# Expert stages of a four-layer kernel in a written order, two blocks a step, with packed constants

## The chip, the cores and the metric

The kernel runs on one core of one Trainium2 chip. The time is the device time of one execution in microseconds. Engines are named as in the profile: PE multiplies matrices (PEld is its weight load), DVE is the vector engine, ACT the activation engine, POOL the general engine that here mostly issues indirect transfers, SP the engine that issues the other transfers. Three runs of the kernel before took 1355.46, 1358.62 and 1359.36 us; the median is 1358.62 us.

## The reference, cut to what matters

Four layers run over `x` of 4 batches, 512 rows and 128 columns, in float32. Each layer adds an attention to `x` and then a mixture of 8 experts:

```
x = x + L0_xattn(layernorm(x), ctx)        # one similarity map, softmax, 512 -> 128 projection
x = x + L0_ffn(layernorm(x))               # top 2 of 8, silu(x W1 + b1) * (x W0 + b0), then W2
x = x + L1_xattn(ctx, ctx, layernorm(x))   # 16 heads of 8 columns, masked
x = x + L1_ffn(layernorm(x))               # top 1 of 8 with a capacity, gelu, hidden 512
x = x + L2_xattn(layernorm(x), ctx)        # 16 heads of 64 columns, own layernorm and a gate
x = x + L2_ffn(layernorm(x))               # top 2 of 8, gelu, hidden 256, no biases
x = x + L3_xattn(layernorm(x), ctx, ctx)   # 16 heads of 64 columns
x = x + L3_ffn(layernorm(x))               # top 2 of 8, relu, hidden 512
```

The context `ctx` has 154 rows for each batch. A softmax runs over these 154 for each of 16 heads and each row of `x`.

## The kernel before

**Tiles.** The rows are cut into 16 tiles of 128 (4 batches `b`, 4 tiles `i` each). `x` stays on the chip for the whole kernel.

**Attention of layers 1 to 3.** `attend_all` (L1272) runs one period for each tile. A period works on two tiles at once: `new`, whose scores, maxima and exponentials are made, and `old`, the tile before it, whose probabilities are turned (transposed), multiplied by the values, scaled, projected and added to `x`. `narrow_period` (L431) is that of layer 1, `wide_period` (L486) that of layers 2 and 3. The pieces are methods of `Tile` (L267). `score(g)` has PE make scores of six heads (four for the last of the three groups) in a two-bank PSUM tile `sc`. `most(g)` has DVE take the maxima of a group (L292). `exp(g)` has ACT do one exponential with a sum for each head (L304). `turn(n)` is four transposes on PE into a tile `tr`, and `take(n)` the copy out of it (L261 on DVE, L264 on ACT). `by_v` is the product with the values, `inverse` (L326) and `replicate` (L331) make the inverse sums, send them through DRAM and read them back spread over the partitions (`rep`), `scaled` (L411) multiplies by them, `project` (L421) and `residual` end the tile. `parts` are the pieces that prepare the next batch (normalised rows, their transpose, keys, values), `queries` the query projection of the next tile. PSUM has two buffers each of `sc`, `tr` and `av`.

**Routing.** `route` (L647) is a generator. For one half of the rows (two batches, 8 tiles) it normalises, makes the logits, finds the top experts and gives each row a place in a buffer of 128-row blocks sorted by expert; it puts the scatters (one indirect transfer on POOL for each tile and choice, L718) on a list, and then makes the weights and adds the last bias. `row_transfers` issues from that list, two for each `take` or block.

**Experts.** `experts` (L821) is a generator too, over 23 blocks for each half (15 in layer 1). For block `j` it reads the expert's number, loads that expert's first weights with its biases packed behind them (`w`, three buffers, L861), multiplies (`up`, L872), and then finishes the block before it (`down`): activation with bias into `hT` (layer 0: ACT's silu into `eg`, L887, then DVE's product, L888; layer 1 L890; layer 2 L880; layer 3 DVE L894 and ACT L896), second product (L899), copy to `ys` (L907) and store to `ybuf`. Every four blocks the next four blocks of tokens are transposed and copied (`tokens`, L845). After a half's blocks, `gather` (L932) fetches rows back from `ybuf` and `combine` (L950) adds them.

**What sets the order.** Within `with tc.manual_schedule(engines=ordered)`, PE, ACT and DVE keep the order in which the program writes their instructions; SP's and POOL's are placed by a planner. Before, only the attention of layers 1 to 3 stands in that block. The attention of layer 0, the expert stages and the routing in them are placed by the planner on all engines. The main loop (L1313 on) steps the generators by turns: blocks of half 0 beside the routing of half 1, then blocks of half 1 beside the combining of half 0 and the preparation of the next attention.

Of the kernel before, what the change touches and what calls it, by code (L numbers as in the profile page):

```python
# [19 lines left out]
P = 128  # L20
# [6 lines left out]
E = 8  # L27
# [19 lines left out]
def tile_xattn_moe_stack(ctx: ExitStack, tc: tile.TileContext, a: dict, out: bass.AP):  # L47
# [94 lines left out]
    wide_ends = const.tile([P, 4, P], F32, name="wide_ends")  # L142
    nc.gpsimd.memset(wide_ends, 0.0)
# [31 lines left out]
    nth = const.tile([1, BLK[0], E], F32, name="nth")  # L175
# [4 lines left out]
    def row_bc(src, n, name):  # L180

        t = const.tile([P, n], F32, name=name)
        nc.sync.dma_start(t, src.partition_broadcast(P))
        return t


    ctxT = const.tile([P, B, S2], F32, name="ctxT")
    ct4 = const.tile([P, B, 4, ST], F32, name="ct4")
    ct2 = const.tile([P, B, 64], F32, name="ct2")
    nc.gpsimd.memset(ct2, 0.0)  # L190
    tp = ps_tr()
    for b in range(B):
        nc.tensor.transpose(tp[:, b * P : (b + 1) * P], cm[:, b, :], ident)
    nc.vector.tensor_copy(ctxT[:, :, 0:P], tp.rearrange("p (b k) -> p b k", b=B))
    tp = ps_tr()
    for b in range(B):
        nc.tensor.transpose(tp[:, b * ST : (b + 1) * ST], ctail[:, b, :], ident[:ST, :ST])
    tpv = tp[:, 0 : B * ST].rearrange("p (b k) -> p b k", b=B)
    nc.vector.tensor_copy(ctxT[:, :, P:S2], tpv)
# [3 lines left out]

    def columns(src, rows, name):

        t = p2.tile([rows, P], F32, tag="rows", name=f"{name}_r")
        nc.sync.dma_start(t, src)
        q = ps_tr()
        nc.tensor.transpose(q[:, 0:rows], t, ident[:rows, :rows])
        o = const.tile([P, rows], F32, name=name)  # L210
        nc.vector.tensor_copy(o, q[:, 0:rows])
        return o
# [54 lines left out]
    class Tile:  # L267
# [8 lines left out]
        def __init__(self, at, i):  # L276
            self.at, self.i = at, i
            self.per = P // at.dh
            self.nb = H // self.per
            self.pr = p2.tile([P, H, S2], F32, tag="probs", name="probs")  # L280
# [31 lines left out]
        def short(self):  # L312
            if self.nb == 1:
                self.ends = p2.tile([P, 4, T4], F32, tag="short", name="short", bufs=1)
                nc.scalar.copy(self.ends.rearrange("p g (h k) -> p (g h) k", h=4), self.pr[:, :, P:S2])
            else:
                self.ends = wide_ends
# [38 lines left out]
        def take_ends(self, engine):  # L356
            self.tails = p2.tile([self.rows, 4, P], F32, tag="tails", name="tails")
            copy(engine, self.tails.rearrange("p g q -> p (g q)"), self.q["ends"][0 : self.rows, :])
# [1028 lines left out]
```

## Time and profile before

| | |
|---|---|
| median of three runs | 1358.62 us |
| profiled execution | 1354.62 us |
| its span, first to last instruction | 1352.8 us |
| mean granted clock of PE | 0.930 |
| PE / PEld busy | 1113.4 / 908.6 us |
| DVE / ACT / POOL busy | 770.9 / 568.8 / 252.9 us |
| transferred | 126.81 MB, mean 94 GB/s |

Read as stages, the span falls into: attention of layer 0 up to 94 us, a wait for scattered rows up to 117, experts of layer 0 up to 293, attention 1 up to about 511, experts 1 up to 605, attention 2 up to about 846, experts 2 up to 955, attention 3 up to about 1199, experts 3 up to 1325, and the last gather up to 1352.8. Busy times of an engine are of its instructions alone; a matmul record's end is modelled.

### The profile page before, as it was taken

The page shows a single profiled execution, that of the slowest core. Times are in us where ns is not written, and L with a number is a line of the kernel's source. Part 1 is how long each engine was busy: PE and PEld are TensorE (multiplying, and loading weights), DVE is VectorE, ACT ScalarE, POOL GpSimd, SP SyncE. Part 2 cuts the span into 40 slices and gives each one's busy share as a digit, 9 for nine tenths or more (in the row PEclk, how much of TensorE's full clock was granted, in tenths as well). Part 3 has the DMA queues.
Part 4 walks back from the last instruction along what each step waited for, and adds up shares of the span by engine and source line. Part 5 has one row for each costly group of instructions (what it writes and reads, how often), then busy time and mean ns, then how long its engine had stood idle before and what let it go on. Part 6 is the DMA issues. An engine that isn't in the chain of part 4 may idle for free.

```text
span 1352.8 us, 26947 instructions
## 1 busy us (share of the span) xinstructions
PE 1113.4 (82%) x9435; PEld 908.6 (67%) x9435; DVE 770.9 (57%) x2089; ACT 568.8 (42%) x2258; POOL 252.9 (19%) x281
## 2 busy tenths in 40 slices
PE   4885988887777788889999988868899998889891
PEld 3775887764334347777778777756777777679881
DVE  5563645557766764245666776425477576646452
ACT  1112443455454444455555455212555555433230
POOL 2022213104000020312000003045120000402424
PEclk8786998999898988998999999879999999989996
DMA  7013675551101214532112213444421111335762
GB/s 216 0 63 107 184 232 153 167 170 40 21 19 28 63 40 112 147 108 79 33 33 55 57 36 105 114 147 129 126 60 43 33 33 33 86 82 146 203 186 61
DMA packets 136995, 126.81 MB, mean 94 GB/s; under 512 B 13466, under 2 KB 116511, under 8 KB 136479
## 3 DMA queue, kind: packets, MB, share of 16 engines
q1 hardware_dynamic: 129695, 110.39, 29.4%
q0 software_dynamic: 7168, 14.69, 3.6%
q8 instruction: 78, 1.28, 0.4%
q14 instruction: 54, 0.44, 0.1%
HBM read 101.31 MB, written 23.72 MB: 92 GB/s over the span
## 4 chain that ended last, share of the span: by engine, by line
PE 35%; DVE 8%; DMA 6%; ACT 4%; issue 4%; POOL 3%; SPq 0%; POOLq 0%; DVEq 0%; ACTq 0%
PE sc L605 5%; PE tr L421 5%; PE av L404 4%; PE tr L367 4%; PE sc L872 4%; DMA w<-in_up 3%; PE av L899 3%; PE sc L590 3%; ACT probs L304 2%; DVE nm L292 2%; PE av L386 2%; DVE pT L261 2%; POOL yg L932 1%; PE sc L554 1%; POOL buf L718 1%
## 5 line engine op out<-in xcount | busy, mean ns | idle before, releaser
L304 ACT ACTIVATE probs<-sc,nm 128x154 f32<-128x154 f32 x768 | 286.1, 404 | 266.1 <-DVE nm L292 265.8
L872 PE MATMUL sc<-tokT,w 128*128 128x128 f32 x1528 | 213.9, 289 | 29.2 <-DMA w<-in_up 22.8
L872 PEld LDWEIGHTS sc<-tokT,w 128*128 128x128 f32 x1528 | 192.9, 200 | 43.3 <-issue 11.4
L899 PE MATMUL av<-w,hT 128*128 x1160 | 175.0, 284 | 11.4 <-DVE hT L888 8.5
L292 DVE TENSOR_REDUCE nm<-sc 128x6 f32<-128x924 f32 x144 | 142.9, 1009 | 68.1 <-PE sc L605 34.0
L304 ACT ACTIVATION_READ_ACCUMULATOR probs<-sc,nm 128x1 f32 x768 | 170.2, 222 | 0.0
L899 PEld LDWEIGHTS av<-w,hT 128*128 128x128 f32 x1160 | 150.4, 194 | 23.0 <-DVE hT L888 12.7
L932 POOL DMA_INDIRECT yg<-ybuf,su x112 | 107.6, 960 | 277.6 <-DVE pT L261 132.6
L261 DVE COPY pT<-tr 128x512 f32<-128x512 f32 x192 | 128.0, 687 | 52.3 <-PE tr L367 49.3
L233 POOL TENSOR_TENSOR rstd<-ve,nhalf 128x4 f32<-128x4 f32 x32 | 32.9, 1030 | 652.7 <-DVE ve L231 598.6
L718 POOL DMA_INDIRECT buf<-xn,su x112 | 108.1, 965 | 163.5 <-DVE eb L741 42.1
L367 PE MATMUL tr<-ident,probs 128*128 128x128 f32 x768 | 117.2, 287 | 13.3 <-DVE pT L261 13.3
L367 PEld LDWEIGHTS tr<-ident,probs 128*128 128x128 f32 x768 | 84.9, 144 | 40.3 <-DVE pT L261 20.4
L404 PE MATMUL av<-pT,vm 128*64 128x128 f32 (+1 forms) x1536 | 104.8, 286 | 7.1 <-DVE pT L261 7.1
L887 ACT ACTIVATE eg<-sc,w 128x128 f32<-128x128 f32 x184 | 66.2, 367 | 94.5 <-DVE hT L888 72.7
L907 DVE COPY ys<-av 128x128 f32<-128x128 f32 x168 | 48.5, 289 | 82.8 <-PE av L899 75.5
L888 DVE SCALAR_TENSOR_TENSOR hT<-sc,w,eg 128x128 f32<-128x128 f32 x184 | 63.0, 348 | 51.2 <-ACT eg L887 48.6
L404 PEld LDWEIGHTS av<-pT,vm 128*64 128x64 f32 (+1 forms) x1536 | 65.0, 128 | 35.9 <-issue 20.5
L605 PE MATMUL sc<-kT,qT 64*128 64x154 f32 x1024 | 85.1, 304 | 3.5 <-ACT probs L304 3.5
L605 PEld LDWEIGHTS sc<-kT,qT 64*128 64x128 f32 x1024 | 69.8, 186 | 13.3 <-ACT probs L304 7.7
L421 PE MATMUL tr<-wo,aT 128*128 128x128 f32 x512 | 67.1, 284 | 9.3 <-ACT tails L264 6.8
L590 PE MATMUL sc<-xnT,wq 128*128 128x128 f32 x512 | 71.0, 296 | 2.9 <-ACT probs L304 2.9
(251 smaller groups left out, 1460.6 us busy)
## 6 DMA issues: line engine op xcount, KB each, us to landing
w<-in_up SPq DMA_DIRECT2D x46, 516.0 KB
w<-in_up SPq DMA_DIRECT2D x76, 258.0 KB
rep<-rd SPq DMA_DIRECT2D x64, 256.0 KB
ybuf<-ys SPq DMA_DIRECT2D x168, 64.0 KB
tok<-buf SPq DMA_DIRECT2D x36, 256.0 KB
w<-in_down SPq DMA_DIRECT2D x3, 2048.0 KB
w<-in_up SPq DMA_DIRECT2D x46, 128.0 KB
buf<-zero SPq DMA_DIRECT2D x2, 1472.0 KB
```

The costliest lines, as they stand in the source:

```text
L261: return nc.vector.tensor_copy(o, i)
L292: nc.vector.tensor_reduce(self.at.heads(self.nm, g, n), self.sc[g][:, :, 0 : n * S2].rearrange("p j (s k) -> p j s k", s=n), AX.X, ALU.max ...
L304: nc.scalar.activation(self.pr[:, h, :], self.sc[g][:, j, s * S2 : (s + 1) * S2], AF.Exp, bias=self.nm[:, h : h + 1], accum_out=self.rs[:, ...
L367: nc.tensor.transpose(q[:, t * P : (t + 1) * P], self.pr[:, h, 0:P], ident)
L404: nc.tensor.matmul(av[rows, cols], v, self.pT[n][:, t, :], start=False, stop=last)
L421: nc.tensor.matmul(o[:, 0:D], self.aT[:, c, :], self.at.wo[:, c, :], start=(c == 0), stop=(c == self.nb - 1))
L590: nc.tensor.matmul(sc[:, c // 4, c % 4 * P : (c % 4 + 1) * P], wq[:, c * P : (c + 1) * P], at.xnT[:, i * P : (i + 1) * P], start=True, sto ...
L605: nc.tensor.matmul(sc[:, j, s * S2 : (s + 1) * S2], at.qT[i][rows, c, :], at.kT[rows, c, :], start=True, stop=True)
L718: ins = nc.gpsimd.indirect_dma_start(out=buf[half], out_offset=bass.IndirectOffsetOnAxis(ap=su[:, t : t + 1], axis=0), in_=xns[t // NI][:, ...
L872: nc.tensor.matmul(dst, w[:, at : at + P], xT, start=True, stop=True)
L899: nc.tensor.matmul(y[:, 0:D], hT[:, fc, :], w2[:, bass.ds(e, 1), fc, :].rearrange("p o d -> p (o d)"), start=(fc == 0), stop=(fc == nf - 1),)
L932: ins = nc.gpsimd.indirect_dma_start(out=yg[:, t, :], out_offset=None, in_=ybuf[half], in_offset=bass.IndirectOffsetOnAxis(ap=su[:, t : t ...
```

## The change

1. All of the main loop after the attention of layer 0 now stands in the block of the written order: the expert stages, the routing beside them, and the preparation of the next attention.
2. `experts` works on steps of two blocks in layers 1 to 3 (one in layer 0). Weights have four buffers of a step and are loaded three steps ahead. In a step the written order is: load, `up` of this step, `down` of the step before with its copy to `ys` (on ACT in layer 0, on DVE otherwise), activation of this step, and every four blocks the token transposes and their copy. In layer 3 the first block's relu is DVE's and the second block's ACT's.
3. Biases are no longer loaded with the weights. `route` picks each block's biases out of a table on the chip, by a mask and sum over experts on DVE. The weights and the last bias of a half become a second generator, `weigh`; for half 1 of layers 0 to 2 it runs in the next attention.
4. Small constants are packed on the host into a few arrays, the context is also passed transposed, and the transposes that made columns of them on the chip are gone.
5. `narrow_period`: the scores and maxima of group 0 of the next tile are made near the end of the period, after `parts` and before `inverse`; both first exponential groups stand together; `after` ends the period.
6. `wide_period`: the projection comes before the turning of the ends, and turn 0 of the new tile is done at the end of its own period with its copy on ACT.
7. Buffers: `probs`, `rep` and `tails` become single (probs in two halves), `w` has four, `hT` four, `ys` two.

```diff
...
         if new:
-            new.score(0)
             new.score(1)
         if old:
             old.turn_ends()
-        if new:
-            new.most(0)
-        if old:
             old.turn(0)
         if new:
             new.most(1)
             new.exp(0)
+            new.exp(1)
         if old:
             old.take_ends("v")
+            old.take(0, "v")
             old.by_v_ends()
-            old.take(0, "v")
             old.turn(1)
             old.take(1, "v")
+        if new:
+            new.score(2)
+        if old:
             old.turn(2)
             old.by_v(0)
             old.by_v(1)
         if new:
-            new.score(2)
-            new.exp(1)
-        if old:
-            old.take(2, "v")
-        if new:
             new.most(2)
             new.exp(2)
         if old:
+            old.take(2, "v")
             old.turn(3)
+            old.by_v(2)
             old.take(3, "v")
-        middle()
-        if old:
-            old.by_v(2)
             old.by_v(3)
             old.scaled(0)
+        middle()
+        parts()
+        if nxt:
+            nxt.score(0)
+            nxt.most(0)
         if new:
             new.short()
             new.inverse()
         queries()
         if new:
             new.replicate()
-        parts()
-        after()
         if old:
             old.project()
             old.residual()
+        after()
...
-            for n in range(3):
+            for n in (1, 2):
                 old.turn(n)
                 old.take(n, "v")
...
             old.by_v(3)
+            old.scaled(1)
         middle()
-        if old:
-            old.scaled(1)
...
             new.replicate()
-            new.turn_ends()
-            new.take_ends("s")
-        after()
         if old:
             old.project()
             old.residual()
+        if new:
+            new.turn_ends()
+            new.take_ends("s")
+            new.turn(0)
+            new.take(0, "s")
+        after()
...
+        if layer != 2:
...
+            begun = rt.tile([P, BLK[0], E], F32, tag="begun", name="begun", bufs=1)
+            nc.vector.tensor_tensor(begun[:, 0:nj, :], bc(first, 1, nj), nth[:, 0:nj, :], ALU.is_le)
+            nc.vector.tensor_tensor(begun[:, 0:nj, :], begun[:, 0:nj, :], past[:, 0:nj, :], ALU.subtract)
+            yield
...
+            for c in range(nc_):
...
+                nc.vector.tensor_tensor(t8[:, 0:nj, :], begun[:, 0:nj, :], bc(biases[layer][:, c, :], 1, nj), ALU.mult)
+                nc.vector.tensor_reduce(r.biases[:, 0:nj, c], t8[:, 0:nj, :], AX.X, ALU.add)
+                if c % 4 == 3 and c < nc_ - 1:
+                    yield
...
+                    if layer == 0:
+                        g = p2.tile([P, P], F32, tag="eg", name="eg", bufs=4)
+                        nc.scalar.activation(g, sc[:, 1, cols], AF.Silu, bias=bcol[:, j, nf + fc : nf + fc + 1])
+                        nc.vector.scalar_tensor_tensor(hT[:, fc, :], sc[:, 0, cols], b0, g, ALU.add, ALU.mult)
+                    elif layer == 1:
+                        nc.scalar.activation(hT[:, fc, :], sc[:, n, cols], AF.Gelu, bias=b0)
+                    elif n == 0:
+                        nc.vector.tensor_scalar(hT[:, fc, :], sc[:, n, cols], b0, 0.0, ALU.add, ALU.max)
+                    else:
+                        nc.scalar.activation(hT[:, fc, :], sc[:, n, cols], AF.Relu, bias=b0)
...
+            row_transfers(
+                2 * per, copy("s" if layer == 0 else "v", ys[:, 0:m, :].rearrange("p n d -> p (n d)"), y[:, 0 : m * D])
             )
...
+        for n, blocks in enumerate(steps):
+            j = blocks[0]
+            load_up(n + 3)
+            sc = up(blocks, ws.pop(n))
             if last:
                 down(*last)
-            last = this
+            last = blocks, activate(blocks, sc)
             if j % 4 == 2 and j // 4 + 1 in loaded:
                 tokens(j // 4 + 1)
                 load(j // 4 + 2)
             yield
...
+    with tc.manual_schedule(engines=ordered):
+        for layer in range(4):
+            if layer:
+                routed, last, weights = attend_all(layer, prepare, found, at, beside)
+            row_transfers()
+            pace = (1, 3, 2, 2)[layer]
+            first = Steps(experts(layer, 0, routed, weights)).step()
+            if last:
+                (narrow_period if layer == 1 else wide_period)(None, last)
+            if layer < 3:
+                prepare = setups[layer + 1]()
+            second = Steps(routing(layer, 1, layer == 3))
+            while not first.done:
+                first.step()
+                second.step(pace)
+            behind = second.finish()
+            row_transfers()
+            got = gather(0, routed, first.result)
+            second = Steps(experts(layer, 1, behind, weights))
+            while rows_due:
+                second.step()
+            second.step()
+            onto = Steps(onward(layer, 0, routed, got, prepare, found))
+            while not second.done:
+                second.step()
+                onto.step(pace)
+            at = onto.finish()
+            beside = Steps(finishing(behind, gather(1, behind, second.result)))
         row_transfers()
```

## Prediction

> **What bounds the kernel now.** I first read busy time by stage. The columns are the stretch and its length in us, then PE, PEld, DVE, ACT and POOL busy with their instructions, PE's granted clock, the DMA share and GB/s.
>
> ```profile
> 117.00:293.00 176.00, 157.20 (x1228) 145.36 (x1226) 96.39 (x320) 75.89 (x198) 33.03 (x34) 0.97 0.58 175
> 293.00:511.00 218.00, 166.22 (x1318) 84.48 (x1319) 147.30 (x334) 111.35 (x537) 28.25 (x29) 0.91 0.15 43
> 511.00:605.00 94.00, 83.26 (x676) 76.17 (x676) 34.98 (x123) 43.01 (x135) 18.42 (x19) 0.95 0.46 130
> 605.00:846.00 241.00, 215.66 (x2154) 179.86 (x2151) 161.21 (x344) 130.96 (x588) 28.14 (x29) 0.99 0.23 56
> 846.00:955.00 109.00, 83.70 (x570) 73.23 (x569) 41.04 (x147) 26.18 (x61) 33.80 (x35) 0.86 0.45 130
> 955.00:1199.00 244.00, 218.52 (x2159) 181.61 (x2157) 160.48 (x341) 130.75 (x587) 35.88 (x37) 0.98 0.22 58
> 1199.00:1325.00 126.00, 115.46 (x940) 107.17 (x940) 63.73 (x220) 34.60 (x107) 31.80 (x33) 0.99 0.59 160
> ```
>
> Experts 0 to 3 take 176, 94, 109 and 126 us, the attentions between them 218, 241 and 244. PE is busy about nine tenths of each except attention 1 and experts 2, where most room is. Then the waits: who waited, for whom, total us, times, longest.
>
> ```profile
> ACT eg L887 <- DVE hT L888: 72.7, 130, 4.0
> ...
> ACT hT L896 <- DVE hT L894: 54.3, 33, 6.0
> ...
> PE tr L845 <- DMA tok<-buf: 33.3, 7, 15.9
> PE tr L331 <- DVE rinv L326: 32.0, 29, 2.9
> PE sc L872 <- DMA w<-in_up: 22.8, 31, 2.2
> PE av L380 <- DVE tails L261: 18.6, 15, 4.7
> ```
>
> The last four are PE's own and can be won or lost directly; 15.9 us of L845 is the wait for scatters before experts 0. The first two show ACT and DVE taking turns on one `sc` tile. The timeline (start, us, engine) shows it in a block of layer 0:
>
> ```profile
> 143.28 0.37 ACT L887 ACTIVATE eg<-sc,w 128x128 f32<-128x128 f32 x1 [0.43 <-DVE hT L888]
> ...
> 143.68 0.35 DVE L888 SCALAR_TENSOR_TENSOR hT<-sc,w,eg 128x128 f32<-128x128 f32 x1 [0.43 <-ACT eg L887]
> ...
> 144.07 0.37 ACT L887 ACTIVATE eg<-sc,w 128x128 f32<-128x128 f32 x1 [0.42 <-DVE hT L888]
> ...
> 145.63 0.29 DVE L907 COPY ys<-av 128x128 f32<-128x128 f32 x1
> ```
>
> A turn takes 144.07 − 143.28 = 0.79 us. The next silu waits for the product although it needs only another column of `sc`. The copy to `ys` at 145.63 is DVE's, slipped in while ACT has the tile.
>
> [...] granted clocks of 0.86 in experts 2 and 0.91 in attention 1, the stages with most idle PE, against 0.98 and 0.99 in attention 3 and 2, agree.
>
> **The change, part by part**, against the profiled execution's 1354.6 us (span 1352.8), 0.3% under the median of 1358.6.
>
> *Experts 0: +14.* In written order ACT does copy n−1 to `ys` before the silus of block n, and that copy waits for the second product, which waits for the last `hT`. A block's loop is: three turns 3 × 0.79, then silu 0.37, gap 0.03, product 0.35: 3.12. From last `hT` to copy 0.24 (142.45 to 142.69 in the timeline). ACT's copy of 128x128: no such row; 128x208 took 0.38 (L319) and DVE's 0.29, so I take 0.30, bounds 0.26 and 0.39. Sum 3.66; 46 blocks 168.5. Before, steady blocks lasted 3.0 to 3.1 (starts 149.41, 152.49, 155.47), PE's own work: 16 records of L872 in 2.0, 8 of L899 in 1.0, a share of the token transposes. Around the loop: routing and bias pieces on DVE beyond the slack left in a block (statistics 2.7, norm 2.2, bias sums of 0.32 + 0.31 each) about 6.5, two starts of a half 5.4, end 1, preparing attention 1 2, PE's clock at the two starts about 6. Together 190 against 176. The new weight ring and `eg`'s four buffers hold nothing here: loads come three steps ahead, and the 6.8 us that PE waited for `w` in this stage go.
>
> *Attention 1: +11.* PE's transpose of the sums (L331, first instruction of `replicate`) now stands behind `most(0)` of the next tile and `inverse` on DVE. The maximum of six narrow heads takes 1.12, the inverse 0.25, and with 0.18 for the passing of signals the wait is 1.55 a tile; before it was 18.3 in 15 tiles of this stage, 1.2: +5 over 15. `parts` and `middle`, DVE pieces of 0.2 to 1.4 us, now stand ahead of L331 too, where PE has little but the scores of group 0 to do: I take 0.5 a tile, +8 (bounds 0 and 20). The weights of half 1 move in, with 3 us of PE's work and waits. At L380 the product of the ends waits for `tails` behind one maximum fewer on DVE, but PE has one group of scores less to cover it: of 18.6 I take a quarter back, −5 (bounds 0 and 18.6). `exp(0)` and `exp(1)` side by side cost nothing while ACT is busy 111 of 218; without that cover a group of six exponentials, 6 × 0.4, would stand in each tile.
>
> *Experts 1: 0.* 30 blocks at 2.0 of PE are 60; tokens 3.7, their waits 5, the old tile's period 8, routing 3.5, in-order stalls 6 (three pieces a step, so a norm on DVE and its transpose on PE fall in one step), next attention's pieces 7.7: 94, as before.
>
> *Attentions 2 and 3: −4 and −10.* Projection ahead of the turning of the ends removes PE's wait for ACT's copy at L421 (4.1 + 0.7 and 2.7 + 1.4), and turn 0, moved to the end of its own period, takes away part of L367's waits for L261 (7.0 and 6.2; I take 2.5 of the one and, no later piece being in the way in layer 3, 6 of the other; bounds 0 and all). Weights of half 1 bring 3 into attention 2. ACT's added 0.585 a tile lies under its idle time (131 of 241).
>
> *Experts 2: −12.* PE's work is 1.0 a block (four records of L872 and four of L899), 46 in all; tokens 5.7, ten token stalls at 0.9, old tile 9, routing 3.5 + 2.5, next attention's pieces 7.7, border of the halves 10 (16 scatters at 0.965 + 0.30 = 1.27 and the landing, half of it hidden), gathers 3: 97 against 109. PE's 9.7 us for `w` go; the 9.7 for tokens mostly stay.
>
> *Experts 3: +14.* 23 steps at 4.0 are 92; tokens 5.7, old tile 9.5, routing 6.5. Ten token stalls: the copy to `tokT` now stands in its queue behind the copy to `ys` (0.40), four relus on DVE (4 × 0.27 = 1.1) or four on ACT (1.45), and the next `up` waits for it: 1.7 on DVE, 2.8 on ACT, 22 in all; in-order waits at the border 5: 140 against 126.
>
> *No charge:* constants and transposed context (the transposes lie before the first rows are normalised; what else goes lies under 23 us of waiting for scatters with PE busy 2.9); biases of half 0 of layer 0 (5 us of DVE under that wait, DVE busy 5.5 of 23); last gather, 16 × 1.27 on POOL with 8 us around, unchanged; transfers, fewer and of double size, DMA share at most 0.59. The single `rep` and `tails` are read before their next writing in the written order. Scatters and gathers go four a step in layers 1 to 3 against two a block: the same rate on POOL. [...]
>
> Sum in order of time: 14 + 11 + 0 − 4 − 12 − 10 + 14 = +13: 1367.6 beside the profiled execution, 1371.6 beside the median. I take 1371.
>
> **Rivals.**
> A, faster: layer 0's block stays bound by PE at 3.1, because ACT's copy doesn't hold the next silu (PE runs a block ahead, so the wait of the copy ends early). Then 46 × (3.66 − 3.1) = 26 and the 6 of the clock go: about 1340. For it: PE was busy 157 of 176. Against: the copy needs the last product, and the chain of turns alone is 3.12. It decides from a block below 3.38 us, where 46 × 0.28 cancels the 13.
> B, slower still: DVE and ACT pieces meet more waits: copy 0.39 (+4), all token copies on ACT (+6), the clock of 0.91 in experts 0 too (+6), in-order stalls of routing doubled (+8): about 1395.
> C, no change: the token stalls of layer 3 hide under the second block's multiplications, at 2 us a block (14 of the 22 go): 1357.
> That the written order isn't kept is no strong rival: in attention, PE's order in the trace is the written one.
>
> **From the numbers to the chances.** Likeliest 1363 to 1390, 0.48; A 0.24; B 0.20; C 0.08. Faster is A, the same C, slower the rest: 0.24, 0.08, 0.68; three runs spread by 0.3%, which is about what a measurement of this kernel can tell from no change. The range 1332 to 1404 reaches over A and B with the bounds of the copy (46 × 0.13 = 6), of half clocks and stalls, and leaves out what lies past either.
>
> **What would show it.** Right: in experts 0, silus of successive blocks start 3.6 to 3.7 apart and ACT's `ys` copy waits for L899 just before a silu; experts 3 has PE waits at L872 for `tokT`; L331 waits longer in attention 1; waits for `w` are gone; L421's waits for `tails` are gone. Wrong: a block of 3.1 in experts 0, an attention 1 below 218, or token transposes without a wait behind them in layer 3.

## The result, and the profile after

The changed kernel took 1399.91 us (median of 4 runs, 1395.04 to 1400.45) against 1357.04 for the kernel before in the same series: a ratio of 1.0316, 95% interval 1.0272 to 1.0360. It is slower, by 43 us, inside the range of the prediction; but 1371 had been forecast, a loss of 12, less than a third of the real one.

The first view is again busy time by stage, of the profile after from experts 0 on, with the columns that the prediction names. A stage of experts here runs from its first token transpose on PE to its last second product.

```profile
109.90:313.80 203.90, 175.38 (x1196) 152.06 (x1197) 96.27 (x312) 79.04 (x237) 34.77 (x36) 0.94 0.47 150
313.80:543.80 230.00, 172.50 (x1352) 90.78 (x1349) 152.48 (x338) 115.71 (x541) 27.16 (x28) 0.90 0.15 40
543.80:643.80 100.00, 82.77 (x633) 74.80 (x633) 33.49 (x120) 36.78 (x128) 19.48 (x20) 0.90 0.41 124
643.80:877.90 234.10, 216.15 (x2195) 182.01 (x2194) 151.72 (x326) 142.17 (x607) 27.24 (x28) 0.99 0.22 57
877.90:979.00 101.10, 75.70 (x551) 67.61 (x551) 39.49 (x136) 20.59 (x56) 34.73 (x36) 0.86 0.50 143
979.00:1216.60 237.60, 218.58 (x2194) 184.59 (x2195) 151.11 (x326) 141.98 (x608) 34.83 (x36) 0.98 0.23 58
1216.60:1370.80 154.20, 120.32 (x915) 113.57 (x915) 64.58 (x225) 28.95 (x97) 32.66 (x34) 0.89 0.44 131
```

The same stages in several profiles give this table (us; the last row is the last gather). The four columns on the right are runs explained below.

| stage | before | after | after, planner | before, ordered | before, new wide period | after, later copy |
|---|---|---|---|---|---|---|
| attention 0 and scatters | 116.5 | 109.9 | 110.7 | 110.4 | 114.7 | 111.0 |
| experts 0 | 176.1 | 203.9 | 162.1 | 255.7 | 177.2 | 179.8 |
| attention 1 | 219.5 | 230.0 | 226.3 | 220.8 | 221.1 | 229.2 |
| experts 1 | 94.6 | 100.0 | 83.7 | 134.3 | 92.5 | 101.6 |
| attention 2 | 239.5 | 234.1 | 234.4 | 241.4 | 227.7 | 235.5 |
| experts 2 | 110.7 | 101.1 | 88.8 | 163.3 | 110.6 | 96.2 |
| attention 3 | 246.7 | 237.6 | 237.8 | 246.3 | 233.6 | 238.0 |
| experts 3 | 119.9 | 154.2 | 114.9 | 193.7 | 120.7 | 150.9 |
| last gather | 29.2 | 27.9 | 27.9 | 28.7 | 28.1 | 28.1 |

Experts 0 and 3 lost 27.8 and 34.3 us, attention 1 10.5, experts 1 5.4; attentions 2 and 3 and experts 2 gained 5.4, 9.1 and 9.6, and the scatters before experts 0 came 6.6 earlier. From the list of waits of the profile after (who waited, for whom, total us, times, longest), waits of PE and of the two engines that had taken turns:

```profile
ACT hT L930 <- DVE hT L928: 92.2, 17, 11.0
...
ACT eg L923 <- DVE hT L924: 65.8, 138, 2.1
...
PE tr L333 <- DVE rinv L328: 39.4, 32, 4.0
...
PE tr L891 <- DMA tok<-buf: 37.9, 3, 22.0
...
PE sc L902 <- ACT tokT L92: 22.4, 14, 3.0
...
PE av L939 <- DVE hT L924: 19.6, 59, 1.0
...
PE sc L902 <- DVE tokT L88: 17.4, 18, 2.8
```

The waits for weights are down to 1.9 us, from 22.8. In their place PE waits 39.8 us for the transposed tokens to be copied (2.3 before) and 19.6 for the products of layer 0. In a block of layer 0, by the timeline of after:

```profile
199.73 0.37 ACT L923 ACTIVATE eg<-sc,bcol 128x128 f32<-128x128 f32 x1
...
202.50 0.35 DVE L924 SCALAR_TENSOR_TENSOR hT<-sc,bcol,eg 128x128 f32<-128x128 f32 x1 [0.43 <-ACT eg L923]
...
202.90 0.49 PE L939 MATMUL av<-w,hT 128*128 x2 [0.30 <-DVE hT L924]
...
203.43 0.27 ACT L264 COPY ys<-av 128x128 f32<-128x128 f32 x1 [0.96 <-PE av L939]
203.59 0.37 ACT L923 ACTIVATE eg<-sc,bcol 128x128 f32<-128x128 f32 x1
```

This is the loop that the prediction described: last product, PE's last pair, ACT's copy, and only then the next silu. It takes 203.59 − 199.73 = 3.86 us, and the median over the 46 blocks, from first silu to first silu, is 3.86 too. In the kernel before it is 3.40, more than the 3.0 to 3.1 that the prediction took from a few blocks.

### The profile page after: what moved, and what is told of

The parts are those of the page before. It is cut to its first block, busy times and chain, and to the rows that moved or that the text cites. A ratio compares the mean times of both kernels' runs of the same rounds, so it can differ in the third digit from the quotient of the medians.

```text
span 1398.7 us, 26416 instructions
## 1 busy us (share of the span) xinstructions
PE 1126.4 (81%) x9420; PEld 918.4 (66%) x9420; DVE 753.3 (54%) x2021; ACT 582.6 (42%) x2326; POOL 253.0 (18%) x281
## 4 chain that ended last, share of the span: by engine, by line
PE 56%; DVE 21%; ACT 9%; issue 7%; DMA 3%; POOL 3%; SPq 1%; POOLq 0%; ACTq 0%; DVEq 0%
PE sc L902 8%; PE tr L369 7%; PE av L939 6%; PE av L406 5%; PE sc L609 5%; PE tr L423 4%; DVE hT L924 4%; ACT eg L923 4%; PE sc L1181 3%; DVE nm L291 3%; PE sc L594 2%; PE av L388 2%; ACT probs L303 2%; POOL buf L730 1%; PE sc L558 1%
## 5 line engine op out<-in xcount | busy, mean ns | idle before, releaser
L902 PE MATMUL sc<-tokT,w 128*128 128x128 f32 x1528 | 222.9, 306 | 47.8 <-ACT tokT L92 22.4
L902 PEld LDWEIGHTS sc<-tokT,w 128*128 128x128 f32 x1528 | 207.2, 217 | 62.1 <-ACT tokT L92 25.7
L939 PE MATMUL av<-w,hT 128*128 x1160 | 175.9, 290 | 23.1 <-DVE hT L924 19.6
L261 DVE COPY pT<-tr 128x512 f32<-128x512 f32 x160 | 107.2, 688 | 51.4 <-PE tr L369 47.8
L369 PE MATMUL tr<-ident,probs 128*128 128x128 f32 x768 | 121.0, 288 | 0.7 <-DVE rT L335 0.7
L924 DVE SCALAR_TENSOR_TENSOR hT<-sc,bcol,eg 128x128 f32<-128x128 f32 x184 | 64.5, 351 | 101.4 <-ACT eg L923 101.3
L923 ACT ACTIVATE eg<-sc,bcol 128x128 f32<-128x128 f32 x184 | 67.9, 369 | 95.5 <-DVE hT L924 65.8
L261 DVE COPY ys<-av 128x256 f32<-128x256 f32 x64 | 26.3, 411 | 150.8 <-PE av L939 143.6
L930 ACT ACTIVATE hT<-sc,bcol 128x128 f32<-128x128 f32 x88 | 25.2, 368 | 120.7 <-DVE hT L928 92.2
```

What stands on the lines that cost most here:

```text
L261: return nc.vector.tensor_copy(o, i)
L369: nc.tensor.transpose(q[:, t * P : (t + 1) * P], self.pr[:, h, 0:P], ident)
L902: nc.tensor.matmul(sc[:, u if nu > 1 else n, fc * P : (fc + 1) * P], w[:, n, (u * nf + fc) * P : (u * nf + fc + 1) * P], xT, start=True, s ...
L923: nc.scalar.activation(g, sc[:, 1, cols], AF.Silu, bias=bcol[:, j, nf + fc : nf + fc + 1])
L924: nc.vector.scalar_tensor_tensor(hT[:, fc, :], sc[:, 0, cols], b0, g, ALU.add, ALU.mult)
L939: nc.tensor.matmul(y[:, n * D : (n + 1) * D], hT[:, fc, :], w2[:, bass.ds(es[j], 1), fc, :].rearrange("p o d -> p (o d)"), start=(fc == 0) ...
```

## The experiments

Each run gives its ratio to the kernel before, measured beside it on the same chip. The changed kernel is "after".

### Experts 0: the copy's place

```diff
-                down(*last)
+                last_y, done = down(*last), last[0]
             last = blocks, activate(blocks, sc)
+            if last_y is not None:
+                store(done, last_y)
```

> The changed kernel with one move: in layer 0 the copy of block n-1 to ys is written behind the silus and products of block n, still on ACT. Theory (the copy, waiting for the second product, holds the next block's silus, so that a block takes 3.12 of turns + 0.58 from the last hT to the copy + 0.16 from copy to silu = 3.86 us): the block falls to about 3.15, experts 0 from 204 to about 171 us, the whole from 1400 to about 1367. Rival (the stage lost to routing and bias pieces on DVE and to pauses that halve the clock): experts 0 stays above 195, the whole above 1390.

Measured 1377.46 us, ratio 1.0166 (1.0121 to 1.0211). Experts 0 fell from 203.9 to 179.8; no other stage moved by more than 5. So the copy's place costs 24 us, and the rival falls; the stage didn't reach 171 (median block 3.27, upper quartile 4.25). Blocks with neither a token copy nor a piece of routing on DVE last 2.9 us on average, those with a piece of routing 4.1.

```diff
-                2 * per, copy("s" if layer == 0 else "v", ys...
+                2 * per, copy("v", ys...
```

> The changed kernel with the copy to ys of layer 0 on DVE instead of ACT, in the same place of the written order. Theory (it is the place in the order that costs): DVE's first product now stands behind the copy, the loop is 0.58 + 0.30 + 0.35 + 3 x 0.79 = 3.6 a block, a gain of 0.25 x 46 = 11: about 1389. Rival (it is ACT's load that costs): the block falls to 3.1 and the whole to about 1367.

Measured 1397.17, ratio 1.0296 (1.0243 to 1.0349). Experts 0 fell by 7.9 to 196.0, median block 3.49; attention 1 was 5.4 longer, so little shows in the whole. The engine matters less than the place, as the theory said; of the 11 us that had been forecast for the stage 7.9 came.

```diff
             sc = ps_sc()
+            gate = ps_tr() if layer == 0 else None
...
-                            sc[:, u if nu > 1 else n, fc * P : (fc + 1) * P],
+                            (gate if u else sc[:, u if nu > 1 else n])[:, fc * P : (fc + 1) * P],
...
-                        nc.scalar.activation(g, sc[:, 1, cols], ...
+                        nc.scalar.activation(g, gate[:, cols], ...
```

> The changed kernel with one difference in layer 0: the product that feeds the silu goes to a PSUM tile of its own (of the tile kind that the transposes use), so that ACT and DVE read two tiles instead of two banks of one. Theory (ACT and DVE take turns because of the shared tile, and three turns of 0.79 are most of the 3.86 us loop): without turns the loop is 0.58 + 0.16 + 4 x 0.39 + 0.38 = 2.7, PE's 3.1 bounds, experts 0 falls from 204 to about 175, the whole to about 1371, though the copy to ys still stands ahead of the silus. Rival (ACT and DVE can't read PSUM at once, or the block is bound by the copy's place alone): experts 0 within 5 us of 204.

Measured 1355.19, ratio 1.0006 (0.9967 to 1.0045): this one edit takes back the whole loss. Experts 0 fell to 164.6, below the kernel before. The timeline of this run:

```profile
184.33 1.06 PE L942 MATMUL av<-w,hT 128*128 x8
...
185.22 1.06 PE L903 MATMUL tr<-tokT,w 128*128 128x128 f32 x8
185.43 0.27 ACT L264 COPY ys<-av 128x128 f32<-128x128 f32 x1 [2.67 <-PE av L942]
185.59 1.15 ACT L926 ACTIVATE eg<-tr,bcol 128x128 f32<-128x128 f32 x4
...
185.99 1.13 DVE L927 SCALAR_TENSOR_TENSOR hT<-sc,bcol,eg 128x128 f32<-128x128 f32 x4 [3.22 <-ACT eg L926]
```

Four silus run in 1.15 us and four products beside them in 1.13, where three turns alone took 2.37 (3 × 0.79). ACT and DVE do read two PSUM tiles at once: from 185.99 to 186.74 both run here. The median block is 2.68. In such a block PE's 24 matmul records follow each other 0.11 us apart without a pause, so this is PE's own pace here, less than the 3.0 to 3.1 that the prediction took for it.

### Experts 3: the token copies

```diff
+            early = layer == 3
+            due = j % 4 == 2 and j // 4 + 1 in loaded
+            if due and early:
+                tokens(j // 4 + 1)
+                load(j // 4 + 2)
             if last:
                 down(*last)
             last = blocks, activate(blocks, sc)
-            if j % 4 == 2 and j // 4 + 1 in loaded:
+            if due and not early:
                 tokens(j // 4 + 1)
```

> The changed kernel with one move in layer 3: every four blocks, the token transposes and their copy are written behind the step's first product and ahead of the second product, its copy to ys and the relus. Theory (the copy to tokT stands behind copy and relus, PE waits 24.3 us in 11 stalls, and the pauses halve PE's clock for some 10 us more): experts 3 falls from 154 to about 122, the whole from 1400 to about 1367. Rival (the stage lost to routing pieces in written order and to the border of the halves): at most 10 us go, the whole stays above 1388.

Measured 1380.33, ratio 1.0179 (1.0134 to 1.0224); experts 3 fell from 154.2 to 133.7. What was removed is seen in the timeline of after:

```profile
1292.94 0.49 PE L891 MATMUL tr<-ident,tok 128*128 128x128 f32 x3
1293.14 0.43 DVE L261 COPY ys<-av 128x256 f32<-128x256 f32 x1 [2.12 <-PE av L939]
1293.48 1.12 DVE L928 TENSOR_SCALAR hT<-sc,bcol 128x128 f32<-128x128 f32 x4
...
1294.71 1.14 ACT L930 ACTIVATE hT<-sc,bcol 128x128 f32<-128x128 f32 x4 [2.43 <-DVE hT L928]
1295.73 0.50 ACT L92 COPY tokT<-tr 128x384 f32<-128x384 f32 x1
...
1296.28 2.05 PE L902 MATMUL sc<-tokT,w 128*128 128x128 f32 x16 [2.85 <-ACT tokT L92]
```

The copy to `tokT` stands behind DVE's relus, because ACT's relus wait for DVE's and ACT's copy stands behind ACT's; DVE's in turn stand behind the copy to `ys`. PE waits 2.85 us. In all PE waited 17.2 + 7.1 = 24.3 us for `tokT` in the stage; with the move 2.1 are left. That gain arrived. Of the further 10 for the clock little did: PE's busy time fell from 120.3 to 117.0, and the stage is 12 us above its forecast. What is left is another wait; PE's waits in experts 3 of this run begin:

```profile
PE tr L821 <- DVE comb L816: 6.7, 1, 6.7
PE tr L891 <- issue: 3.9, 2, 2.0
PE sc L902 <- DVE tokT L88: 2.1, 3, 0.8
```

By the timeline of this run the combined weights stand on DVE behind 3.0 us of bias sums (1266.50 to 1269.53), and then behind the copy and the relus of a step. The next run spreads them:

```diff
-                if c % 4 == 3 and c < nc_ - 1:
+                if c % 2 == 1 and c < nc_ - 1:
                     yield
...
+            yield
             cTs = []
```

> The changed kernel with the token transposes of layer 3 ahead of the second product and the routing pieces spread (two bias columns a piece, a step between combined weights and their transposes). If the pause of 6.7 us for the combined weights and the half clock behind it are what is left of experts 3's loss, the stage falls from 133.7 to about 127, PE's busy time from 117.0 to about 114. If the pieces only move the pause, it stays above 131.

Ratio 1.0104 (0.9999 to 1.0209); the stage is at 128.1, PE busy 114.7: as the theory said. (This run and the next are of two executions each, on a chip where the kernel before took 1351.24 us.) In the other stages of after PE waits only 1.7 us in all for combined weights. Spreading has a price: attention 2 takes 240.8 here, 234.1 in after.

Filling the pauses on PE (a pure addition, read by nobody) asks for the clock's share:

```diff
             evac(toks[g][:, 0 : m * P], q[:, 0 : m * P])
+            if layer == 3 and 0 < g:
+                q = ps_tr()
+                for c in range(12):
+                    nc.tensor.transpose(q[:, (c % 4) * P : (c % 4 + 1) * P], ident, ident)
```

> The changed kernel with twelve more transposes of the identity, read by nobody, written behind each token transpose of layer 3 after the first: 1.5 us of PE work inside pauses of 0.8 to 3.0 us. If pauses at the token copies are what halves the clock in experts 3, PE's busy time less the added 10 times 1.5 falls from 120.3 to about 114 and the stage by some 5 us, from 154 to 149. If the clock is halved by other pauses (start of a half, combined weights), busy time less the added stays at 120 and the stage is at 154 to 157.

Ratio 1.0323 (1.0234 to 1.0412). The stage went to 152.2, and busy time, less 120 transposes at 0.12 by my estimate (matmul records are 0.11 apart in the timeline of split0), from 120.3 to 115.8: between the two forecasts. By that, the half clock behind the pauses at the token copies makes some 4 of the 12 us by which the same 915 instructions of PE are busy longer than in the run with the planner below (120.3 against 108.4). The other pauses were not filled singly, but the trace says where they are. PE's clock in after is at full or at half and holds one value for 3.41 us or, but for one of 66 stretches, a whole multiple of it. Ten such windows of the stage are at half there: four behind pauses for `tokT`, two behind the combined weights, two at the stage's start, one in the pieces of routing (from 1247 on), one at the border of the halves. This run's clock of 0.91 over the stage is that of eight, and its longest wait for `tokT` is 1.7 us.

```diff
-                    elif n == 0:
+                    elif fc < 2:
```

Here two columns of each block go to DVE and two to ACT.

> The changed kernel with the relus of layer 3 shared as in the kernel before: in each block two columns on DVE and two on ACT, instead of a block each. Theory (DVE and ACT take turns on the one sc tile in either case and the sum of a step's relus, 4 x 0.27 + 4 x 0.36, is the same): within 4 us of 1400. Rival (the sharing by blocks is what costs in experts 3): 10 us or more go.

Measured 1415.16, ratio 1.0426 (1.0363 to 1.0489): both theories missed. Experts 3 grew by 14 to 168.3. A step's relus, in four turns, take 2.70 us (1303.81 to 1306.51 in this run's timeline), in two turns 2.37 (1293.48 to 1295.85 above), PE's wait for `tokT` rose from 24.3 to 31.1, and its busy time from 120.3 to 126.4. Sharing the relus by blocks was a gain within this order.

### Attention: each period alone

The period of attention 1 as before, in after:

```diff
-    def narrow_period(new, old, nxt=None, ...):   [the changed body]
+    def narrow_period(new, old, nxt=None, ...):   [the body of before]
...
-        if layer == 1:
-            new.score(0)
-            new.most(0)
```

> The changed kernel with the period of attention 1 as it was before (group 0 of a tile scored and its maxima taken at the start of its own period), everything else as changed. Theory (the transpose of the sums at replicate stands behind the next tile's maxima, pieces of the next batch and the inverse): attention 1 falls from 230 to about 219 us, the whole from 1400 to about 1389. Rival (attention 1 is longer by the weights and the last bias of half 1, which moved into it, whatever the order of the period): within 4 us of 1400.

Measured 1397.56, ratio 1.0305 (1.0226 to 1.0383); attention 1 at 228.6, from 230.0. The numbers are the rival's, but its reason, the weights of half 1, was not tried alone. Nor is the period's order cleared: attention 1 took 235.4 and 235.9 us in two runs that leave it as in after (the copy on DVE, the token move), so that 6 us there are within what changes by itself, and in a later pair the old period is 6.8 shorter. From the last second product of experts 0 to the first transpose of the sums passed 6.9 us before and 13.1 after; the periods between took 211.3 and 214.0. So 6 of the 10.5 us lie at this entry, where before the planner had put the first scores under the end of the experts. With the planner around the new periods (next section) the entry is 10.4: less than half of the 6 is the written order's.

The period of attentions 2 and 3 alone, in the kernel before:

```diff
-            for n in range(3):
+            for n in (1, 2):
...
-            new.turn_ends()
-            new.take_ends("s")
-        after()
         if old:
             old.project()
             old.residual()
+        if new:
+            new.turn_ends()
+            new.take_ends("s")
+            new.turn(0)
+            new.take(0, "s")
+        after()
```

> The kernel before with only the period of attentions 2 and 3 as changed (projection ahead of turning the ends, turn 0 at the end of its own period with its copy on ACT); expert stages, routing and constants as before. Theory (the gain in attention 2 and 3, 5.4 and 9.1 us, comes from this order alone): attention 2 at about 232 (nothing of the weights of half 1 is in it here), attention 3 at about 237, the whole 13 to 17 us below the kernel before, about 1339. Rival (it comes from what the written order of the stages around brings): within 5 us of the kernel before.

Measured 1325.06, ratio 0.9766 (0.9694 to 0.9839): a gain of some 32 us, twice the forecast (27 between the two profiled executions). Before, PE waited in attention 2 for 7.0 us at L367 behind the probabilities' copies and 4.1 at L421 behind ACT's copy of the ends:

```profile
PE tr L367 <- DVE pT L261: 7.0, 15, 1.8
...
PE tr L421 <- ACT tails L264: 4.1, 6, 0.7
```

Neither is in the list of this run, which begins:

```profile
PE tr L331 <- DVE rinv L326: 6.3, 7, 2.3
```

Attentions 2 and 3 fell by 11.8 and 13.1 us here, and by 5.4 and 9.1 in after: the entries there, 15.5 and 16.8 us, are 4.0 and 5.9 longer than before.

### The written order itself

Only the attention's periods in written order, all else of the change kept:

```diff
-    with tc.manual_schedule(engines=ordered):
+    if True:
         for layer in range(4):
...
+        with tc.manual_schedule(engines=ordered):
             new = Tile(at, 0, probs[:, 0])
```

> The changed kernel with one part undone: only the periods of attention stand in the block of the written order, as before; expert stages, routing and preparation are placed by the planner again, with the steps of two blocks, the packed constants and the changed periods kept. Theory (the written order of the expert stages is what costs: ACT's copy ahead of the silus, token copies behind the relus, routing pieces ahead of PE's next work, and no score of the next attention ahead of the last second product): experts 0 about 178, experts 3 about 125, the starts of the attentions 4 to 6 us shorter, the whole about 1330. Rival (steps of two blocks and four buffers cost, whatever the order): above 1375.

Measured 1288.72, ratio 0.9514 (0.9465 to 0.9562). This is 111 us below after and 5% below the kernel before. All of the stages of experts gain (table above): 41.8, 16.3, 12.3 and 39.3. The change without its first part is worth 68 us, and its first part costs 111. The theory had 70 of these. Where it was wrong is the starts of the attentions: the entries are 10.4, 15.2 and 15.7 us here and 13.1, 15.5 and 16.8 in after, and attentions 2 and 3 are as long as in after. So what lengthens those two against the run with the new wide period alone is not the written order around them; which other part of the change it is was not tried.

The written order alone, in the kernel before:

```diff
-        with tc.manual_schedule(engines=ordered):
+        if True:
             for b in range(B):
...
-    for layer in range(4):
+    with tc.manual_schedule(engines=ordered):
+        for layer in range(4):
```

> The kernel before with the written order alone carried over its expert stages, nothing else changed: blocks one at a time, biases loaded with the weights, old periods. Theory (order alone costs): in layer 0 the first product of a block stands behind DVE's copy to ys, so 3.6 a block and experts 0 about 196; experts 3 about 140; the attentions start 4 to 6 us later each: the whole about 1410. Rival (the order costs only with the changed steps and with the copy on ACT): within 15 us of the kernel before.

Measured 1595.64, ratio 1.1741 (1.1684 to 1.1797): more than four times the loss that had been expected (239 us against 54). The waits name a place that the theory had not:

```profile
PE sc L872 <- DMA w<-in_up: 136.9, 91, 6.1
```

Here a block's weights are loaded in its own turn; before, this wait was 22.8 us in all. In after they are loaded three steps ahead and 1.9 us are left, which suggests that part 2 of the change is what made the order bearable. Loads ahead without the rest of the change were not tried.

Then the order on PE alone, and on ACT and DVE alone, in the stages of experts of after. These two and the last two of the next section were on a chip on which the kernel before took 1463.39 us; a comparison of their ratios with those of other chips is rough.

```diff
                 routed, last, weights = attend_all(layer, prepare, found, at, beside)
+            with tc.manual_schedule(engines={mybir.EngineType.PE}):
...
```

> The changed kernel with the expert stages, routing and preparation in written order on PE alone; ACT and DVE there are placed by the planner, the attention stays in written order. Theory (the copies and activations on ACT and DVE, held behind each other, are what costs; PE's written order is near its natural one): experts 0 below 175, experts 3 below 130, the whole near 1310. Rival (PE's order costs: products of routing and the next scores held behind waiting second products): above 1360.

```diff
+            with tc.manual_schedule(engines={mybir.EngineType.Activation, mybir.EngineType.DVE}):
```

> The counterpart: written order on ACT and DVE alone in the expert stages, PE placed by the planner there. Theory (order on ACT and DVE costs): experts 0 above 190, experts 3 above 140, the whole above 1360. Rival (PE's order costs): near 1310.

Ratios 0.9716 (0.9650 to 0.9782) and 0.9935 (0.9915 to 0.9955), between 0.9514 with neither and 1.0316 with both, which are of another chip: 2.0 points for PE, 4.2 for ACT and DVE, 8.0 for both. Read so, ACT and DVE's order costs twice as much as PE's, and the two together more than their sum. The excess over the sum is not shown, though. On this same chip the planner with a split tile in layer 0 (next section) took 1365.46 us; with the 13.7 us added by which experts 0 are shorter there than without the split (148.4 against 162.1, on two chips), the kernel with neither would take about 1379, by my estimate, and the two orders would cost 44 and 75 us, 3.0 and 5.1 points, whose sum is about the 8.0 of both. The difference between the two lies in layer 0: with ACT and DVE in order experts 0 took 203.9 us and the median block was again 3.86, with PE alone 170.7 and 3.16. In experts 1 to 3 together they are 36 and 31 us longer than that planner run.

### Versions that put the findings together

These combine edits shown above, as their expectations say; the token move there is for all layers.

> The changed kernel with the copy to ys of layer 0 behind the silus, the token transposes ahead of the second product in all layers, the period of attention 1 as before, and the pieces of routing spread (two bias columns a piece, and a step between the combined weights and their transposes, for which PE waited 6.7 us behind bias sums). Theory (the losses add): experts 0 about 180, attention 1 220, experts 1 and 2 97, attention 2 and 3 235 and 238, experts 3 about 126, the whole about 1335, some 20 us below the kernel before. Rival (one loss hides another, the border of the halves and the half clock keep their share): not below the kernel before.

Measured 1343.24, ratio 0.9916 (0.9886 to 0.9945). Experts 3 at 127.3, attention 1 at 219.4, experts 0 at 179.4: as expected. The whole is 8 us above the forecast; attention 2, at 240.6, has 6 of them.

> The changed kernel with the silu's input in a tile of its own in place of the later copy, and the other three edits kept: token transposes ahead of the second product in all layers, the period of attention 1 as before, the pieces of routing spread. Theory (the losses add, and the split frees more than the later copy did): experts 0 about 165, attention 1 220, experts 1 to 3 95, 100 and 127, attention 2 and 3 238 each: about 1323. Rival (the split tile meets the early token transposes in the same two buffers): experts 0 above 180, the whole at 1340.

Measured 1318.67, ratio 0.9711 (0.9667 to 0.9754); experts 0 at 154.6.

> The kernel before with the changed period of attentions 2 and 3 and, in layer 0, a PSUM tile of its own for the silu's input. Theory (before, PE bounds a block at 3.0 to 3.1 with turns of 3.12 close behind, so little is left for the split): experts 0 from 177 to 168 or so, the whole from 1325 to about 1317. Rival (the planner's order and the transposes' buffers, one of which the tile takes, undo it): not below 1325.

Measured 1305.91, ratio 0.9626 (0.9585 to 0.9666); experts 0 at 156.7, from 177.2: twice the gain expected. The turns had bounded the block before as well.

> The changed kernel with its expert stages placed by the planner, and the silu's input of layer 0 in a PSUM tile of its own. Theory (the turns of 0.79 are still near the bound of a block): experts 0 from 162 to about 154, the whole from 1289 to about 1280. Rival (PE's 3.0 a block is the bound, 46 x 3.0 = 138 with the rest of the stage unchanged): within 3 us of 1289.

Ratio 0.9338 (0.9289 to 0.9386); experts 0 at 148.4. The theory's step, some 9 us, is exceeded, as far as two chips can be compared.

> As the run before it (planner, split tile), with the period of attention 1 as it was before. Theory of the prediction (the new narrow period makes PE wait longer at the sums' transposes): attention 1 from 226 to about 219 and the whole about 7 lower. Rival (the weights of half 1 in the first periods are what costs there, whatever the order): within 3 us of the run before it.

Ratio 0.9299 (0.9250 to 0.9347). Attention 1 was 6.8 us shorter than in the run before it, attention 2 4.3 longer; the intervals overlap, so which narrow period is better outside the order is not settled. These last two are the fastest seen, 7% below the kernel before.

## Why the prediction was right and wrong

**Right in direction and in mechanism, wrong in the size of two terms.** Both losses that it named are there: ACT's copy ahead of the silus, and token copies behind the relus. But the two stages lost 62 us where 28 had been forecast. Attention 2, attention 3 and experts 2 came within 3 us of −4, −10 and −12, the first two in part by luck (below), and the waits for weights went as forecast.

**Experts 0: +14 forecast, +27.8 measured.** The term that failed is "From last `hT` to copy 0.24 (142.45 to 142.69 in the timeline)". That product belongs to the next block. The timeline of before shows it:

```profile
141.78 0.33 DVE L888 SCALAR_TENSOR_TENSOR hT<-sc,w,eg 128x128 f32<-128x128 f32 x1
...
142.12 0.33 DVE L888 SCALAR_TENSOR_TENSOR hT<-sc,w,eg 128x128 f32<-128x128 f32 x1
...
142.28 0.19 PEld L899 LDWEIGHTS av<-w,hT 128*128 128x128 f32 x1
...
142.69 0.29 DVE L907 COPY ys<-av 128x128 f32<-128x128 f32 x1 [0.24 <-PE av L899]
```

The last weight load of the second product begins at 142.28, before the product at 142.12 has ended at 142.45, so it can't be waiting for it. The product before, begun at 141.78 and 0.33 long, is the right one: 142.69 − 142.11 = 0.58, exactly what after shows (202.85 to 203.43). On the other side, ACT's next silu starts 0.16 after the copy does, not 0.30. The loop is 3.12 + 0.58 + 0.16 = 3.86 instead of 3.66, and 46 × 0.20 = 9 of the 14 us missed; the rest lies in what stands around the loop, 26 where 21 had been taken.

**Experts 3: +14 forecast, +34.3 measured.** The waits for `tokT` were right, 24.3 against 22. The term "in-order waits at the border 5" was too small: PE stood idle 33.9 us in all in the stage (154.2 − 120.3), where 27 had been counted, with 4.2 for combined weights and 2.0 at the border. And PE's work was taken at full clock, 114 in the sum, while it was busy 120.3 at a granted clock of 0.89. The kernel before had 1.00 here. The prediction charged the clock in experts 0 and put it at nothing in experts 3. These two make some 14 of the 20 us missed; the other 6 come from where the stage is taken to begin and end, since the prediction's stage before was 126 us long and this one is 119.9.

What a pause on PE does to its clock is seen in the trace of after. A wait of 2.83 us ended at 1236.93 and the clock was halved behind it; a wait of 2.85 us ended at 1296.28 and it was not:

```profile
1237.00:1240.00 3.00, 3.00 (x15) 3.00 (x16) 2.83 (x15) 0.00 (x0) 1.65 (x2) 0.52 0.04 13
1296.30:1300.00 3.70, 3.70 (x33) 3.70 (x34) 0.00 (x0) 0.00 (x0) 0.00 (x0) 1.00 0.48 142
```

Counted on from the steps of the clock in windows of 3.41 us, the first pause lies inside one window (1233.74 to 1237.15), the second across the border of two (at 1295.18), with 1.75 and 1.10 us in each. In the whole trace of after, all 21 windows at full clock in which PE had neither matmul nor weight load for more than 1.95 us were followed by the half clock; of the 269 with less than 1 us, four were.

**Experts 1: 0 forecast, +5.4 measured.** PE's work was as taken, 82.8 us busy against 83 in the sum. Its idle time was 17.2, where the sum had 11 for waits and stalls (10.5 before): among them 7.4 at the token transposes and 5.0 for `tokT`, which had been 0.8.

**Attention 1: +11 forecast, +10.5 measured, by the wrong step.** The wait at L331 grew only from 19.3 to 26.4 us, by 7.1, where 13 had been taken, and giving the old period back gained 1.4, within what this stage changes by itself. The entry, which the sum did not have, is 6 of it. The right total was luck.

**Attention 2 and 3.** The step was right, its size not: the new period alone gains 25 us in the two, where 14 had been forecast with 3 of weights in it, and in after 10 of the 25 are lost again, about as much as the entries grew. Why the entries grew stays open; with the planner around they are nearly as long. That these two errors cancel is luck.

**Nothing forecast, 6.6 us gained** in the scatters before experts 0. The kernel before with the order alone, whose constants are as they were, has 110.4, and the changed kernel with the planner there, which keeps the packing, 110.7. Runs that are alike up to there spread from 103.4 to 111.0, so the cause stays open.

**Rivals.** A, the block at PE's pace, did not come; its decision point was stated rightly (3.38 us; measured 3.86). But it held a wrong belief, that 3.1 is PE's pace: with the turns gone the block is 2.68. B came nearest in time, through the right terms in part (half clocks, stalls of routing), not through the copy, which was shorter than taken.

**What the sum lacked** is a look at the parts apart. Every estimate compared a stage with itself before, and so a loss of 111 and a gain of 68 were never seen. The place of a `with` alone is what separates 1400 us from 1289, and a PSUM tile alone takes 45 of the 1400.

## What to carry to other kernels

A written order cost time here where an instruction stood behind one that waited (24 us for ACT's copy in experts 0, 20.5 for the token copies in experts 3), and what it cost was seen by following one loop round through the engines: last producer, consumer, copy, next start. Match every instruction of the loop to its block before taking a difference; a weight load that began 0.17 us before a producer had ended was enough here to refuse a wrong match. Two engines that shared a PSUM tile took turns of 0.79 us here though each read its own half of it, and giving each its own tile was worth more than moving the copy (39 us of experts 0 against 24); and a change of several parts is best priced with and without its largest part.

## What the runs showed of the hardware that had not been expected

PE's pace was better read here from spacing than from durations: in split0 eight matmul records of 128x128 that the timeline joins to 1.06 us begin 0.11 apart, and a block of 24 ran in 2.68 us, though its three groups sum to 3.2. A pause of 2.83 us was followed by the half clock where it lay inside one window of 3.41 us, and one of 2.85 by the full clock where it lay across two; more than 1.95 us without work in one window were followed by the half clock in all 21 cases of after.
